# A decoder layer's retention: column-tiled products in one run per chunk, state in f16 halves, weight rows loaded a job ahead

## The chip, the cores and the metric

The kernel runs on one core of a Trainium2 chip, in one launch. The metric is the device time of an execution in microseconds, as a median over runs. The core has a matmul engine (TensorE; PE in the profile, with its weight loads as PEld) and three engines for elementwise work: VectorE (DVE), ScalarE (ACT) and GpSimd (POOL). SyncE (SP) issues nearly all DMAs, in order. Each engine takes its instructions in the order in which the program holds them and waits on semaphores for the others.

## The reference, cut to what matters

One decoder layer over x of 4 sequences of 1024 tokens, 512 wide: causal attention with head gates, then retention over a context, then a feed-forward with faked 8-bit quantisation; each is added to its input and normalised. The change concerns the second part.

```python
def _L0_xattn_ref(query, key, value, W_Q, W_K, W_V, g_w, g_b, out_w, out_b):
    q = jnp.einsum('bld,hde->bhle', query, W_Q)
    k = jnp.einsum('bld,hde->bhle', key, W_K)
    v = jnp.einsum('bld,hde->bhle', value, W_V)
    q = _xpos(q, downscale=False)
    k = _xpos(k, downscale=True)
    sim = jnp.einsum('bhnd,bhsd->bhns', q, k) * _decay_mask(L, H)[None]
    ret = jnp.einsum('bhns,bhsd->bhnd', sim, v)
    mu = ret.mean(axis=-1, keepdims=True)
    var = ret.var(axis=-1, keepdims=True)
    ret = (ret - mu) / jnp.sqrt(var + GN_EPS)
    ret = ret.transpose(0, 2, 1, 3).reshape(B, L, D)
    gate = jax.nn.silu(query @ g_w.T + g_b)
    return ret * gate @ out_w.T + out_b

x = _layernorm(x + _L0_attn_ref(x, ...))
x = _layernorm(x + _L0_xattn_ref(x, ctx, ctx, ...))
x = _layernorm(x + _L0_ffn_ref(x, ...))
```

`_decay_mask` is gamma to the power n - s on and below the diagonal, with one gamma for each of 16 heads of 32 columns.

## The kernel before

It has three parts, one after the other on the same core. The **attention** (`main`, `coarse`, `proj` and others) takes batch by batch, four groups of four heads each. The **retention** takes the 4096 tokens in 16 units of 256 tokens, each of two chunks of 128. The **feed-forward** first multiplies by the gate and up weights, then by the down weights; those weights are quantised during the retention.

Precision comes from pairs: a value is split into a high and a low f16 half, and a product is three f16 matmuls (`mm3g`, lines 196 to 198: high by high, high by low, low by high). Some products take f32 operands instead.

*A retention chunk* (`core`, line 999). For each of four groups `o` of four heads: four f16 score products `pst` (L1018), k and q stacked as three parts of 32 rows; a causal mask on DVE, which writes `sm` in f32 (L1020); and, one group later, `intra`: one f32 product of the carried state with `qtf`, the f32 copy of the transposed q (L1008), and four column-tiled f32 products, one for each head, `vv` against `sm` (L1012). Column-tiled means that each writes 32 of the 128 output partitions (`tile_position`). All of a chunk goes to one PSUM bank, `po`, which ACT copies to `rf` (L1040). The new state is `pkv` = k by v (L1029), plus the old state on DVE (L1034), times the decays on POOL (L1035).

*The tail of a chunk*: `tail_a` transposes `rf`, forms the norm over each head (with a power on POOL, L1059) and multiplies by the gate; `tail_b` multiplies by the output weights, adds the residual row `r` (loaded at L1047 into one of `NRB` = 4 buffers), normalises and stores (L1086).

*The projections of the next unit* (`stage1`: `kv`, then `qg`): k and v from the context, rotation tables on DVE and POOL, transposes to `kt` and `qt`. `q_trans` copies its PSUM tile to `qtf` on ACT (L335), then to the f16 high half (L336), and DVE forms the low half (L337). `k_stack` and `q_stack` write the halves to DRAM (`khl_d`, `qhl_d`, L263) and read them back stacked, in three loads each (`sk`, L266).

*Weight jobs* (`wjobs`, line 1088): 38 jobs that quantise the feed-forward weights. Each loads its row block into `fw`, one buffer (L1093, L1105), takes the maximum on DVE (L1095, L1111), quantises on ACT (L1126), casts, transposes on PE, copies and stores.

The order of the work is made by `gmerge`: each stream of work yields an estimated cost after each piece, divided by the stream's weight (`W_CORE`, `W_S1`, `W_F`, `W_TA`...), and the stream that is least far along emits its next piece. A scheduler in the build then settles the order on each engine. Tiles with the same tag share buffers; a new tile waits until the old one in its buffer has been read. `together` adds a dependence, so that a group of column-tiled matmuls isn't started before its last input is there; the attention already uses it.

Of the kernel before, what the change touches and what calls it, by code (L numbers as in the profile page):

```python
# [18 lines left out]
P = 128  # L19
# [11 lines left out]
XS = 1024.0  # L31
MS = 256.0
KEEP = 5
NHS = 6
# [23 lines left out]
WB = 16e3  # L58
TW = 0.307
QW = 15125.0  # L60
# [9 lines left out]
ATLP = 0  # L70
NRB = 4
X_S = 215.2
# [3 lines left out]
WBY = 250  # L76
X_P = 151.7
D_NM = 163.1
W_PR = 20760.0
W_G = 8800.0  # L80
W_X = 10160.0
W_S = 10250.0
W_BE = 11480.0
W_F = 2293.0
W_S1 = 33600.0
W_CORE = 5199.0
W_TA = 1605.0
D_TA = 504.8
# [49 lines left out]
def decoder_kernel(ctx: ExitStack, tc: tile.TileContext, a, c, out):  # L138
# [102 lines left out]
    ktab = []  # L241
    qtab = xp.tile([P, NT, 2, HD // 2], F32, name="qtab")
    etab = xp.tile([P, H], F32, name="etab")
    cmask = xp.tile([P, P], F32, name="cmask")
    FULL = [P, H, HD // 2, 2]
# [62 lines left out]
    def q_tiles(u, tiles):  # L308
        s = un[u]
        s.update(tiles)  # L310
        s["qtf"] = xp.tile([P, KC, UT], F32, tag="suf", name="qtf", bufs=2)
        s["sg"] = {}
# [9 lines left out]
    def q_proj(u, t, ps, **mm):  # L322
        s = un[u]
        p = ps.tile([P, 512], F32, name="pq", **mm)
        yield from mm3g(p, [lambda k, i_=i_: s["xs"][t][:, i_, k, :] for i_ in range(2)], [lambda k, w_=w_: w_[:, k, :] for w_ in bw[2]], KC, 213)
        cs = [qtab[:, tt(u, t), i, None, :].unsqueeze(3).to_broadcast(FULL) for i in range(2)]
# [22 lines left out]
    with ExitStack() as es:  # L349
# [64 lines left out]
        nc.vector.tensor_scalar_mul(ident_m, ident, -1.0 / MS)  # L414
        bsel = cp.tile([3, 3, P], F32, name="bsel")
        tiny = cp.tile([P, 1], F32, name="tiny")
# [59 lines left out]
        def gates(bs):  # L476
            n = len(bs)
            hid = wk_.tile([P, 8, 4], F32, tag="g_hid", name="g_hid", bufs=1)[:, :, 0:n]
            xw = wk_.tile([P, KC, 32], F32, tag="g_xw", name="g_xw", bufs=1)
            nc.gpsimd.memset(xw, 0.0)  # L480
# [340 lines left out]
        def weights_b():  # L821
# [17 lines left out]

            for t, nm in ((qtab, "qtab"), (etab, "etab"), (cmask, "cmask")):  # L840
                nc.sync.dma_start(out=t, in_=c[nm])
# [110 lines left out]
    with ExitStack() as es:  # L952
# [46 lines left out]
        def core(u, t):  # L999
            s = un[u]  # L1000
            kk, vv, qtf, ksk, qsk = (s[k] for k in ("kk", "vv", "qtf", "ksk", "qsk"))
            first, last = tt(u, t) == 0, tt(u, t) == NT - 1
            state = carry.get("state")
            po = ps.tile([P, KC, P], F32, tag="po", name="po", bufs=1)

            def intra(o, sm):
                if not first:
                    nc.tensor.matmul(po[:, o, :], lhsT=state[:, o, :], rhs=qtf[:, o, tk(t)], start=True, stop=False)  # L1008
                with tc.high_priority():
                  for h in range(4):  # L1010
                    r = slice(32 * h, 32 * h + 32)
                    nc.tensor.matmul(po[r, o, :], lhsT=vv[:, t, o * P + 32 * h:o * P + 32 * h + 32], rhs=sm[:, h, :], start=first, stop=True, tile_position=(0, 32 * h))  # L1012

            prev = None
            for o in range(KC):
                pst = ps.tile([P, 4, P], F32, tag="st", name="pst", bufs=2)
                for h in range(4):
                    nc.tensor.matmul(pst[:, h, :], lhsT=ksk[:, h, o, tk(t)], rhs=qsk[:, h, o, tk(t)], start=True, stop=True)  # L1018
                sm = wk_.tile([P, 4, P], F32, tag="sm", name="sm", bufs=NSM)
                nc.vector.tensor_tensor(out=sm, in0=pst, in1=cmask[:, None, :].to_broadcast([P, 4, P]), op=ALU.mult)  # L1020
                yield 213
                if prev is not None:
                    intra(*prev)
                    yield 480
                prev = (o, sm)
            if not last:
# [6 lines left out]
                else:  # L1033
                    nc.vector.tensor_tensor(out=ns, in0=pk, in1=state, op=ALU.add)  # L1034
                    nc.gpsimd.tensor_tensor(out=ns, in0=ns, in1=maskg, op=ALU.mult)  # L1035
                carry["state"] = ns
                yield 853
            intra(*prev)
            rf = s["rf", t] = wk_.tile([P, KC, P], F32, tag="rf", name="rf", bufs=2)
# [27 lines left out]
        def tail_b(u, t):  # L1067
# [18 lines left out]
            nc.sync.dma_start(out=x2_d[ti * P:(ti + 1) * P, :], in_=r)  # L1086

        def wjobs():
# [9 lines left out]
            for o in range(KC):  # L1098
                w3 = wk_.tile([P, 3], F32, tag="wm3", name="wm3")
                wm = wk_.tile([P, 1], F32, tag="wm", name="wm")  # L1100

                def load(o, j):
                    n = min(512, I - 512 * j)
                    w = wk_.tile([P, D], F32, tag="fw", name="fw", bufs=1)
                    nc.sync.dma_start(out=w[:, :n], in_=a["w_down"][o * P:(o + 1) * P, 512 * j:512 * j + n])  # L1105
                    return w, n

                def bound(o=o, w3=w3, wm=wm):
                    for j in range(3):
                        w, n = load(o, j)  # L1110
                        nc.vector.tensor_reduce(out=w3[:, j:j + 1], in_=w[:, :n], axis=AX.X, op=ALU.max, apply_absolute_value=True)  # L1111
                    nc.vector.tensor_reduce(out=wm, in_=w3, axis=AX.X, op=ALU.max)
                yield bound
                for j in range(3):
                    def job(o=o, j=j, wm=wm):
                        w, n = load(o, j)
                        wfinish(w, wm, 2 * NI + o, n, lambda pt_sb: nc.sync.dma_start(out=wT_d["w_down"][:, 4 * j:4 * j + n // P, o * P:(o + 1) * P], in_=pt_sb[:, :n // P, :]))
# [234 lines left out]
def _constants():  # L1352
# [25 lines left out]
    c["ktab"] = ktab.reshape(NT, P, 2, D // 2).transpose(1, 0, 2, 3).astype(f)  # L1378
    c["etab"] = (EPS * gam[None, :] ** (-2.0 * p[:, None])).astype(f)
    mg = np.zeros((P, KC, P), f)  # L1380
# [48 lines left out]
```

## Time and profile before

| | us |
|---|---|
| runs of the kernel | 1962.6, 1973.27, 1976.05 |
| median | 1973.27 |
| the profiled execution | 1978.85 |
| its span, first to last instruction | 1977.1 |
| mean granted TensorE clock | 0.979 |

The profile is of one execution. Line numbers (L1012) are those of the kernel before; `out<-in` names tiles; "x8" counts records that follow each other. An f32 matmul of 128 columns leaves two records, an f32 transpose one. Records of matmuls overlap, since matmuls are pipelined: the cost of one is read from its start to the start of the next. Busy time of 40 slices of the span, in tenths, shows the three parts:

```profile
PE   7689899999999999998889999999999999799996
DVE  4567766677766777678886777787777767798888
ACT  5655555555555555555553323333223322454375
POOL 1075566756667656766553455445554545200066
```

The retention is the stretch from the 22nd digit to the 34th, where ACT is least busy.

### The profile page before, as it was taken

The page shows a single profiled execution, that of the slowest core. Times are in us where ns is not written, and L with a number is a line of the kernel's source. Part 1 is how long each engine was busy: PE and PEld are TensorE (multiplying, and loading weights), DVE is VectorE, ACT ScalarE, POOL GpSimd, SP SyncE. Part 2 cuts the span into 40 slices and gives each one's busy share as a digit, 9 for nine tenths or more (in the row PEclk, how much of TensorE's full clock was granted, in tenths as well). Part 3 has the DMA queues.
Part 4 walks back from the last instruction along what each step waited for, and adds up shares of the span by engine and source line. Part 5 has one row for each costly group of instructions (what it writes and reads, how often), then busy time and mean ns, then how long its engine had stood idle before and what let it go on. Part 6 is the DMA issues. An engine that isn't in the chain of part 4 may idle for free. (4 is left out here: it accounts for less than half of the span.)

```text
span 1977.1 us, 34827 instructions
## 1 busy us (share of the span) xinstructions
PE 1832.6 (93%) x13456; PEld 968.2 (49%) x13456; DVE 1455.4 (74%) x2455; ACT 918.2 (46%) x1496; POOL 1015.4 (51%) x962
## 2 busy tenths in 40 slices
PE   7689899999999999998889999999999999799996
PEld 4444445444445444554434555555555555344432
DVE  4567766677766777678886777787777767798888
ACT  5655555555555555555553323333223322454375
POOL 1075566756667656766553455445554545200066
PEclk9899999999999999999999999999999999899999
DMA  9612222212123112223137454454545444561076
GB/s 272 192 45 67 82 73 68 84 60 81 54 68 97 62 55 65 73 81 129 44 95 223 136 149 139 147 158 134 153 143 150 120 120 144 176 231 34 0 240 229
DMA packets 149720, 231.00 MB, mean 117 GB/s; under 512 B 34479, under 2 KB 58674, under 8 KB 148914
## 3 DMA queue, kind: packets, MB, share of 16 engines
q1 hardware_dynamic: 148978, 227.72, 38.0%
q8 instruction: 106, 1.74, 0.4%
q10 hardware_dynamic: 576, 1.05, 0.1%
q14 instruction: 60, 0.49, 0.1%
HBM read 156.89 MB, written 71.70 MB: 116 GB/s over the span
## 5 line engine op out<-in xcount | busy, mean ns | idle before, releaser
L693 POOL TENSOR_TENSOR acc<-acc,pt 128x384 f32<-128x384 f32 (+3 forms) x436 | 441.0, 1042 | 244.5 <-ACT pt L707 146.2
L637 DVE TENSOR_REDUCE m<-pco 128x2 f32<-128x1024 f32 (+3 forms) x384 | 356.9, 950 | 128.5 <-PE pco L636 71.3
L707 ACT ACTIVATE pt<-pst 128x1024 f32<-128x1024 f32 (+3 forms) x320 | 240.6, 766 | 179.5 <-PE pst L706 102.4
L633 PE MATMUL pco<-kst,qst 96*128 96x512 f16 (+3 forms) x768 | 186.0, 332 | 28.6 <-DMA qst<-qhl_d 15.7
L703 PE MATMUL pst<-qst,kst 97*128 97x512 f16 (+3 forms) x768 | 187.6, 331 | 9.1 <-DVE m L637 4.9
L1324 POOL TENSOR_TENSOR r<-r,xt 128x512 f32<-128x512 f32 x28 | 38.4, 1383 | 196.2 <-DVE r L1321 186.6
L688 PE MATMUL av<-pt,v 128*32 128x512 f32 (+3 forms) x1280 | 131.0, 482 | 8.7 <-ACT pt L707 7.9
L633 PEld LDWEIGHTS <-qst 96*128 96x128 f16 x768 | 63.7, 99 | 120.2 <-issue 83.7
L1059 POOL TENSOR_TENSOR rs<-var,neghalf 128x16 f32<-128x16 f32 x32 | 93.6, 2925 | 46.9 <-DVE var L1057 26.4
L703 PEld LDWEIGHTS <-kst 97*128 97x128 f16 x768 | 59.4, 98 | 104.0 <-issue 83.2
L1253 PEld LDWEIGHTS <-slab_c 128*128 128x128 bf16 x704 | 68.3, 98 | 78.4 <-issue 1.4
L196 PE MATMUL pqk<-xh,slab_a 128*128 128x512 f16 x256 | 97.1, 384 | 8.7 <-ACT xh L399 5.9
L693 DVE TENSOR_TENSOR acc<-acc,pt 128x512 f32<-128x512 f32 (+3 forms) x102 | 96.5, 963 | 8.7 <-POOL acc L693 4.7
L197 PE MATMUL pqk<-xl,slab_a 128*128 128x512 f16 x256 | 98.0, 383 | 0.0
L198 PE MATMUL pqk<-xh,slab_a 128*128 128x512 f16 x256 | 97.8, 382 | 0.0
L196 PE MATMUL pkv<-slab_b,ch 128*128 128x512 f16 x256 | 97.0, 379 | 0.4 <-DVE dn L732 0.4
L197 PE MATMUL pkv<-slab_b,ch 128*128 128x512 f16 x256 | 97.0, 379 | 0.0
L198 PE MATMUL pkv<-slab_b,cl 128*128 128x512 f16 x256 | 97.0, 379 | 0.0
L1256 ACT ACTIVATE sl<-pw_gate,sgx 128x512 f32<-128x512 f32 x88 | 60.1, 684 | 76.3 <-PE pw_gate L1253 74.7
L196 PE MATMUL pv<-slab_a,xh 128*128 128x128 f16 x512 | 92.0, 221 | 3.4 <-ACT slab_a L170 2.4
L197 PE MATMUL pv<-slab_a,xh 128*128 128x128 f16 x512 | 92.0, 221 | 1.2 <-DVE slab_a L171 1.2
L1020 DVE TENSOR_TENSOR sm<-pst,cmask 128x512 f32<-128x512 f32 x128 | 85.3, 679 | 10.5 <-PE pst L1018 9.2
(299 smaller groups left out, 4595.7 us busy)
## 6 DMA issues: line engine op xcount, KB each, us to landing
xt<-x_d SPq DMA_DIRECT2D x63, 256.0 KB, 3.1
xf<-in_xT_dram SPq DMA_DIRECT2D x48, 256.0 KB, 2.8
kst<-khl_d SPq DMA_DIRECT2D x48, 256.0 KB, 4.0
qst<-qhl_d SPq DMA_DIRECT2D x96, 128.0 KB, 3.8
sk<-qhl_d SPq DMA_DIRECT2D x48, 256.0 KB, 3.8
sk<-khl_d SPq DMA_DIRECT2D x48, 256.0 KB, 4.0
khl_d<-khl SPq DMA_DIRECT2D x16, 512.0 KB, 2.8
xr<-in_x_dram SPq DMA_DIRECT2D x32, 256.0 KB, 2.7
```

The costliest lines, as they stand in the source:

```text
L196: nc.tensor.matmul(ps, lhsT=lh(k), rhs=rh(k), start=k == 0, stop=False)
L197: nc.tensor.matmul(ps, lhsT=lh(k), rhs=rl(k), start=False, stop=False)
L198: nc.tensor.matmul(ps, lhsT=ll(k), rhs=rh(k), start=False, stop=k == n - 1)
L633: nc.tensor.matmul(p[:, j, :n], lhsT=qst[0:96, half, h + j, i * P:(i + 1) * P], rhs=ks[0:96, h + j, 512 * part:512 * part + n], start=True ...
L637: nc.vector.tensor_reduce(out=m[:, h:h + 2, i, 1 - half + part], in_=p[:, :, :n], axis=AX.X, op=ALU.max)
L688: together(nc.tensor.matmul(av[32 * h:32 * h + 32, lo:], lhsT=v[:, kt, 32 * h:32 * h + 32], rhs=pt[:, h, lo:], start=kt == 0, stop=kt == n ...
L693: last["acc"] = eng.tensor_tensor(out=acc[:, h:h + hb, lo:], in0=acc[:, h:h + hb, lo:], in1=pt[:, h:h + hb, lo:], op=ALU.add)
L703: nc.tensor.matmul(p[:, j, lo:], lhsT=ks[:, h + j, kt * P:(kt + 1) * P], rhs=qst[:, g, h + j, lo:], start=True, stop=kt < 4 * g)
L707: last[kt] = nc.scalar.activation(pt[:, h:h + 2, lo:], p[:, :, lo:], AF.Exp)
L1020: nc.vector.tensor_tensor(out=sm, in0=pst, in1=cmask[:, None, :].to_broadcast([P, 4, P]), op=ALU.mult)
L1059: nc.gpsimd.tensor_tensor(out=rs, in0=var, in1=neghalf, op=ALU.pow)
L1253: nc.tensor.matmul(p, lhsT=wT[nm][:, k, i * P:(i + 1) * P], rhs=xqT[g][:, k, :], start=k == 0, stop=k == KC - 1)
```

## The change

Its core:

```diff
+VS = 16.0
-TW = 0.307
+TW = 0.2345
-NRB = 4
+NRB = 3
-X_P = 151.7
-D_NM = 163.1
+X_P = 219.7
+D_NM = 211.1
-W_X = 10160.0
+W_X = 15000.0
-W_F = 2293.0
-W_S1 = 33600.0
-W_CORE = 5199.0
-W_TA = 1605.0
+W_F = 1773.0
+W_S1 = 22680.0
+W_CORE = 12560.0
+W_TA = 3398.0
...
-        cl = xp.tile([P, KC, UT], F16, tag="qk32", name="cl", bufs=2)
+        cl = xp.tile([P, KC, UT], F16, tag="qk32", name="cl")
...
-        nc.scalar.activation(un[u]["vv"][:, t, :], p, AF.Copy, scale=1.0 / XS)
+        nc.scalar.activation(un[u]["vv"][:, t, :], p, AF.Copy, scale=VS / XS)
...
-        nc.scalar.copy(s["qtf"][:, :, tk(t)], pt)
         nc.scalar.copy(qh, pt)
...
-                f = xp.tile([P, 512], F32, tag="qk32", name="qk32", bufs=2)
+                f = wk_.tile([P, 512], F32, tag="xr", name="qk32", bufs=2) if b == 0 and ot < 3 else xp.tile([P, 512], F32, tag="qk32", name="qk32")
...
-            def intra(o, sm):
-                if not first:
-                    nc.tensor.matmul(po[:, o, :], lhsT=state[:, o, :], rhs=qtf[:, o, tk(t)], start=True, stop=False)
-                with tc.high_priority():
-                  for h in range(4):
-                    r = slice(32 * h, 32 * h + 32)
-                    nc.tensor.matmul(po[r, o, :], lhsT=vv[:, t, o * P + 32 * h:o * P + 32 * h + 32], rhs=sm[:, h, :], start=first, stop=True, tile_position=(0, 32 * h))
-            prev = None
+            sms = []
             for o in range(KC):
                 pst = ps.tile([P, 4, P], F32, tag="st", name="pst", bufs=2)
                 for h in range(4):
                     nc.tensor.matmul(pst[:, h, :], lhsT=ksk[:, h, o, tk(t)], rhs=qsk[:, h, o, tk(t)], start=True, stop=True)
-                sm = wk_.tile([P, 4, P], F32, tag="sm", name="sm", bufs=NSM)
-                nc.vector.tensor_tensor(out=sm, in0=pst, in1=cmask[:, None, :].to_broadcast([P, 4, P]), op=ALU.mult)
+                if o == 0:
+                    sm2 = xp.tile([P, 2, 4, P], F32, tag="suf", name="sm2", bufs=2)
+                sm = sm2[:, o] if o < 2 else wk_.tile([P, 4, P], F32, tag="sm", name="sm", bufs=NSM)
+                masked = nc.vector.tensor_tensor(out=sm, in0=pst, in1=tab["mask"][:, None, :].to_broadcast([P, 4, P]), op=ALU.mult)
+                sms.append(sm)
                 yield 213
-                if prev is not None:
-                    intra(*prev)
-                    yield 480
-                prev = (o, sm)
+            if not first:
+                for o in range(KC):
+                    for i, (x_, y_) in enumerate(((0, 0), (0, 1), (1, 0))):
+                        nc.tensor.matmul(po[:, o, :], lhsT=state[1][:, x_, o, :], rhs=qt[:, y_, o, tk(t)], start=o == 0 and i == 0, stop=False)
+                yield 640
+            with tc.high_priority():
+                for o in range(KC):
+                    for h in range(4):
+                        r = slice(32 * h, 32 * h + 32)
+                        together(nc.tensor.matmul(po[r, o, :], lhsT=vv[:, t, o * P + 32 * h:o * P + 32 * h + 32], rhs=sms[o][:, h, :], start=first, stop=first or o == KC - 1, tile_position=(0, 32 * h)), masked)
...
+                nh = wk_.tile([P, 2, KC, P], F16, tag="state16", name="state16")
+                nc.scalar.copy(nh[:, 0], ns)
+                nc.gpsimd.tensor_tensor(out=nh[:, 1], in0=ns, in1=nh[:, 0], op=ALU.subtract)
+                carry["state"] = ns, nh
...
+        def fetch():
+            src = next(loads, None)
+            if src:
+                w = wk_.tile([P, D], F32, tag="fw", name="fw", bufs=2)
+                nc.sync.dma_start(out=w[:, :src[1]], in_=src[0])
+                loaded.append((w, src[1]))
+        def take():
+            if not loaded:
+                fetch()
+            w = loaded.pop(0)
+            fetch()
+            return w
...
-                        w = wk_.tile([P, D], F32, tag="fw", name="fw", bufs=1)
-                        nc.sync.dma_start(out=w, in_=a[nm][i * P:(i + 1) * P, :])
+                        w, _ = take()
```

In words: `qtf` and its copy go; the state is kept in f32 for the recurrence and also as two f16 halves, and its product with q becomes three f16 products that add into the same bank; the sixteen column-tiled products of a chunk come last, in one run, tied to the last mask. `vv` is scaled by 16, and the constant table of the norm's epsilon by its square. Weight rows get two buffers, and a job's load is issued a job ahead; `loads` lists the blocks in the order in which the jobs take them. The space comes from tables that take over buffers of the attention's gates (`bsel`, `g_xw`), from `NRB`, and from `qk32`, which keeps one of two buffers; the masked scores of the first two groups go where `qtf` was (`suf`). `W_S` changes too, but no stream uses it.

More of the change, by code (lines that the diff above doesn't have):

```diff
@@ L76 @@
 WBY = 250
-X_P = 151.7
-D_NM = 163.1
+X_P = 219.7
+D_NM = 211.1
 W_PR = 20760.0
 W_G = 8800.0
-W_X = 10160.0
-W_S = 10250.0
+W_X = 15000.0
+W_S = 10990.0
 W_BE = 11480.0
-W_F = 2293.0
-W_S1 = 33600.0
-W_CORE = 5199.0
-W_TA = 1605.0
+W_F = 1773.0
+W_S1 = 22680.0
+W_CORE = 12560.0
+W_TA = 3398.0
 D_TA = 504.8
@@ L241, in decoder_kernel @@
     ktab = []
-    qtab = xp.tile([P, NT, 2, HD // 2], F32, name="qtab")
+    tab = {}
     etab = xp.tile([P, H], F32, name="etab")
-    cmask = xp.tile([P, P], F32, name="cmask")
     FULL = [P, H, HD // 2, 2]
@@ L310, in q_tiles @@
         s.update(tiles)
-        s["qtf"] = xp.tile([P, KC, UT], F32, tag="suf", name="qtf", bufs=2)
         s["sg"] = {}
@@ L325, in q_proj @@
         yield from mm3g(p, [lambda k, i_=i_: s["xs"][t][:, i_, k, :] for i_ in range(2)], [lambda k, w_=w_: w_[:, k, :] for w_ in bw[2]], KC, 213)
-        cs = [qtab[:, tt(u, t), i, None, :].unsqueeze(3).to_broadcast(FULL) for i in range(2)]
+        cs = [tab["q"][:, tt(u, t), i, None, :].unsqueeze(3).to_broadcast(FULL) for i in range(2)]
         xpos(p, cs[0], cs[1], s["qq"][t])
@@ L414, in decoder_kernel @@
         nc.vector.tensor_scalar_mul(ident_m, ident, -1.0 / MS)
-        bsel = cp.tile([3, 3, P], F32, name="bsel")
+        bsel = xp.tile([3, 3, P], F32, tag="bsel", name="bsel")
         tiny = cp.tile([P, 1], F32, name="tiny")
@@ L478, in gates @@
             hid = wk_.tile([P, 8, 4], F32, tag="g_hid", name="g_hid", bufs=1)[:, :, 0:n]
-            xw = wk_.tile([P, KC, 32], F32, tag="g_xw", name="g_xw", bufs=1)
+            xw = xp.tile([P, KC, 32], F32, tag="g_xw", name="g_xw")
             nc.gpsimd.memset(xw, 0.0)
@@ L838, in table @@
                 ktab.append(t)
-            for t, nm in ((qtab, "qtab"), (etab, "etab"), (cmask, "cmask")):
+            tab["q"] = xp.tile([P, NT, 2, HD // 2], F32, tag="bsel", name="qtab")
+            tab["mask"] = xp.tile([P, P], F32, tag="g_xw", name="cmask")
+            for t, nm in ((tab["q"], "qtab"), (etab, "etab"), (tab["mask"], "cmask")):
                 nc.sync.dma_start(out=t, in_=c[nm])
@@ L1000, in core @@
             s = un[u]
-            kk, vv, qtf, ksk, qsk = (s[k] for k in ("kk", "vv", "qtf", "ksk", "qsk"))
+            kk, vv, qt, ksk, qsk = (s[k] for k in ("kk", "vv", "qt", "ksk", "qsk"))
             first, last = tt(u, t) == 0, tt(u, t) == NT - 1
@@ L1033, in core @@
                 else:
-                    nc.vector.tensor_tensor(out=ns, in0=pk, in1=state, op=ALU.add)
+                    nc.vector.tensor_tensor(out=ns, in0=pk, in1=state[0], op=ALU.add)
                     nc.gpsimd.tensor_tensor(out=ns, in0=ns, in1=maskg, op=ALU.mult)
-                carry["state"] = ns
+                nh = wk_.tile([P, 2, KC, P], F16, tag="state16", name="state16")
+                nc.scalar.copy(nh[:, 0], ns)
+                nc.gpsimd.tensor_tensor(out=nh[:, 1], in0=ns, in1=nh[:, 0], op=ALU.subtract)
+                carry["state"] = ns, nh
                 yield 853
-            intra(*prev)
             rf = s["rf", t] = wk_.tile([P, KC, P], F32, tag="rf", name="rf", bufs=2)
@@ L1086, in tail_b, with wloads @@
             nc.sync.dma_start(out=x2_d[ti * P:(ti + 1) * P, :], in_=r)
+        def wloads():
+            for nm in ("w_gate", "w_up"):
+                for i in range(NI):
+                    yield a[nm][i * P:(i + 1) * P, :], D
+            for o in range(KC):
+                for _ in range(2):
+                    for j in range(3):
+                        n = min(512, I - 512 * j)
+                        yield a["w_down"][o * P:(o + 1) * P, 512 * j:512 * j + n], n
+        loads, loaded = wloads(), []
+        def fetch():
[10 more added lines that the diff above has]
+            return w
         def wjobs():
@@ L1100, in wjobs, with bound @@
                 wm = wk_.tile([P, 1], F32, tag="wm", name="wm")
[L1102 to L1108, printed above, removed]
+                def bound(w3=w3, wm=wm):
                     for j in range(3):
-                        w, n = load(o, j)
+                        w, n = take()
                         nc.vector.tensor_reduce(out=w3[:, j:j + 1], in_=w[:, :n], axis=AX.X, op=ALU.max, apply_absolute_value=True)
@@ L1115, in job @@
                     def job(o=o, j=j, wm=wm):
-                        w, n = load(o, j)
+                        w, n = take()
                         wfinish(w, wm, 2 * NI + o, n, lambda pt_sb: nc.sync.dma_start(out=wT_d["w_down"][:, 4 * j:4 * j + n // P, o * P:(o + 1) * P], in_=pt_sb[:, :n // P, :]))
@@ L1378, in _constants @@
     c["ktab"] = ktab.reshape(NT, P, 2, D // 2).transpose(1, 0, 2, 3).astype(f)
-    c["etab"] = (EPS * gam[None, :] ** (-2.0 * p[:, None])).astype(f)
+    c["etab"] = (EPS * VS * VS * gam[None, :] ** (-2.0 * p[:, None])).astype(f)
     mg = np.zeros((P, KC, P), f)
```

## The prediction

> **What bounds the kernel now.** I read the totals first, then the three stretches of the span that the two stage borders cut out (1062.6 us: first score product `pst` of the retention; 1703.5 us: the matmul `pmax` that opens the feed-forward), then the waits of TensorE in the middle stretch, then its instructions in order of time.
>
> ```profile
> PE 1832.6 (93%) x13456; PEld 968.2 (49%) x13456; DVE 1455.4 (74%) x2455; ACT 918.2 (46%) x1496; POOL 1015.4 (51%) x962
> ```
> ```profile
> 0.00:1062.60 1062.60, 975.47 (x7749) 497.85 (x7750) 747.52 (x1126) 580.49 (x985) 630.38 (x636) 0.98 0.31 91
> 1062.60:1703.50 640.90, 613.25 (x4513) 358.07 (x4512) 472.79 (x901) 190.10 (x322) 319.92 (x267) 0.98 0.48 142
> 1703.50:1977.10 273.60, 243.90 (x1196) 112.27 (x1195) 235.10 (x428) 147.60 (x189) 65.09 (x59) 0.96 0.47 158
> ```
> Columns: length, busy us of PE, weight loads, DVE, ACT, POOL, then granted clock, DMA share, GB/s. The retention (second row) is where nearly all of the change lies: PE is busy 96% of it, DVE 74%, POOL 50%, ACT 30%. So a PE slot saved there shortens the span, and work moved to ACT or POOL has room. What PE waits for there:
>
> ```profile
> PE po L1012 <- DVE sm L1020: 5.8, 6, 2.2
> PE pst L1018 <- DMA sk<-qhl_d: 4.4, 4, 1.9
> PE pout L196 <- ACT zh L170: 4.1, 6, 1.2
> ```
> Total us, times, longest. These are small; the stage is a queue of matmuls. The slots, from three places of the timeline (start, length, group):
>
> ```profile
> 1213.89 0.39 PE L1008 MATMUL po<-qtf,state 128*128 128x128 f32 x2
> 1214.21 0.43 PE L1012 MATMUL po<-sm,vv 128*32 128x128 f32 x8
> 1214.57 0.49 PE L1008 MATMUL po<-qtf,state 128*128 128x128 f32 x2
> ```
> ```profile
> 1230.61 1.04 PE L318 MATMUL ptx<-ident,x 128*128 128x128 f32 x8
> 1231.58 0.65 PE L1012 MATMUL po<-sm,vv 128*32 128x128 f32 x16
> 1232.16 0.39 PE L196 MATMUL pout<-wo,zh 128*128 128x512 f16 x1
> ```
> ```profile
> 1440.87 0.38 PE L1008 MATMUL po<-qtf,state 128*128 128x128 f32 x2
> 1441.09 0.38 PE L196 MATMUL pkv<-slab_b,ch 128*128 128x512 f16 x1
> 1452.82 0.61 PE L1018 MATMUL pst<-sk 96*128 96x128 f16 x8
> 1453.26 0.38 PE L196 MATMUL pgt<-wg,xs 128*128 128x512 f16 x1
> ```
> Lengths overlap, so I use start to start. One f32 state product (two records) takes 1441.09-1440.87 = 0.22 us. Eight f16 products of 128 columns, each with its own weight load, take 0.44: 0.055 each. A column-tiled group of four heads (8 records) starts at 1214.21, though the state product before it ends its slot at 1213.89+0.22 = 1214.11, and lets the next start at 1214.57: 0.45 in all (two decimals; over all 116 such groups the median is 0.451). Two groups in one run (16 records): 0.67 from the end of the transposes (1230.61 plus eight of 0.11) to 1232.16. So a further group in a run costs 0.22, and entering and leaving the tiled mode 0.23.
>
> **The change part by part.**
>
> Column-tiled runs. Before: 116 single groups and 6 doubles, 116x0.451 + 6x0.668 = 56.3 us. In the changed program's instruction order all 32 chunks have their 16 tiled matmuls next to each other: 32x(0.23+4x0.2185) = 35.4. Saved: **-20.9**, all of it PE slots.
>
> State products. Before 112 f32 at 0.22: 25.0 us. After 336 f16 (high by high, high by low, low by high) at 0.055 to 0.057 (the 128x128 f16 products `pv` of the attention average 0.057 with a load each): 19.0. **-6.0**. Bound above: if no load overlapped, the 0.098 us of the load record each, 32.9, +8; I take the f16 rows, the same shape beside the same work.
>
> The Trainium skill ("TensorE: Matmul & The Clock Gate", section Back-to-back issue gap) speaks against this part: it gives about 81 ns for a sustained load-and-matmul pair of 128 columns. By it the estimate for the states would be 336x0.081 = 27.2, a loss of 2 instead of a gain of 6; the slot of 55 ns on the `pst` row above decides.
>
> Masks. A run now waits for the mask of the last of its four score tiles (`together`), and everything behind it in PE's order waits too. In the new order 3.5 to 6.0 us of other matmuls stand between that score product and the run in 30 chunks (before, per group, 0.7 to 21.8); the last two chunks have 0.9 and 0.2. The trace puts the mask's end 1.65 us (median) after its product, 4.2 at nine in ten. So of the 5.8 us waited now I let 2 go: **-2** (bounds -5 to +8, a quarter us per chunk).
>
> Recurrence. Product `pkv`, DVE add, POOL mask, and now an ACT copy to f16 and a POOL subtract (28 of each: about 0.59 and 1.27 us, by rows of those engines at 128x512). Before, state is ready 3.0 us after `pkv`; now about 5.0. PE has 5.6 to 18 us of other matmuls before the first state product of the next chunk, so the new wait is covered: **+0.5**. If one 2.9-us `rs` power (L1059) stands before the subtract on POOL, 7.9 against those distances leaves ten chunks short, +10; nothing below zero, since nothing waited here. What is queued behind a late state product is all of PE. ACT loses the 32 `qtf` copies (0.58 each) and gains 28: free.
>
> Hand-over of q. Before a unit's first score product, `qt` goes to DRAM and back in three loads `sk`:
>
> ```profile
> 1339.73 0.37 SPq L263 DMA_DIRECT2D qhl_d<-qt  x1
> 1344.62 0.52 SPq L1096 DMA_DIRECT2D w_up_d<-fs  x1
> 1345.23 1.54 SPq L266 DMA_DIRECT2D sk<-qhl_d  x3
> ```
> From the last q transposition to the last landing it takes 10.5 us (unit 11: 1499.2 to 1509.7), 11.6 (unit 2), 12.9 (unit 5), 14.6 (unit 15); the lines show why: the store was issued at 1339.73 and takes 2.8, but SP's queue held the loads until 1345.23 behind a weight store. Other units had their product after 10.4 to 11, so 11.3 is typical. The dropped `qtf` copy stood first on ACT: 10.7 from now on. The redrawn weights let the projections (W_S1 33600 to 22680) come later beside the core (W_CORE 5199 to 12560): the matmuls that cover the hand-over shrink from 9.8-12.0 us to 8.1, 8.5, 10.7, 11.1, 11.3, 10.6, 10.0, 9.7, 10.9, 11.2, 11.3, 10.4, 10.9, 11.2, 9.4 in units 1 to 15. What is short of 10.7 adds up to 8.2, less 4.4 waited now: **+4** (bounds -4.4, and +34 at 12.9 less 0.6 rounded up).
>
> Weight rows ahead. DVE waited 34.9 us for `fw` (25.2 before L1095, 9.7 before L1111). DVE is no bound; the PE waits that come after its weight work are 2.2 us. I take **-1** (0 to -10). Loads on SP keep their number; with two buffers each waits for a quantisation a job back.
>
> Tail. The last chunk's masks end, then 1.1 us of tiled matmuls instead of 0.45 go before the copy that starts the last norm: **+0.7**.
>
> Attention. Its stream weights (W_X, X_P, D_NM) shift single instructions by up to 3 us of PE work, the gates by 15 earlier; totals stay. `qk32` loses a buffer: a write would wait for the subtract before it. In the trace 6 of the projections after the first three heads start 0.3 to 0.7 us before that subtract ends, 2.6 us together, on ACT. **0** (bounds -4 and +4). The tables' new tags belong to tiles that the gates use last, at 206 us; the tables are loaded near 1000. `NRB` 3: in both instruction orders a residual row's load stands 1 to 6 places behind the store that frees its buffer on SP, so no new kind of wait comes; the load is one chunk later, and POOL, which already waits 84.5 us for these rows (L1048), may hold the state's steps behind it: inside the +10 of the recurrence.
>
> Sum: -20.9-6.0-2+0.5+4-1+0.7 = -24.7. The profiled execution took 1978.85 us (span 1977.1 and 1.75 around it): 1954.1. The median of the runs is 5.6 lower, so I forecast **1948 us**.
>
> **The rivals.** (1) *Much of it goes into the hand-over*: at 11.5 us the covers above fall 17.2 short, +13 instead of +4, and with the recurrence at half its bound (+5): 1948+9+4.5 = 1962. For: SP blocks, and DVE serves the low half late. Against: 11.3 is today's typical value with `qtf` in it. (2) *Slower: the hand-over becomes the clock of each unit.* If SP's order, one queue for weight rows ahead, residual rows and `sk`, brings every unit to what unit 15 shows, 13.9 without `qtf`, the shortfall is 53.2, +48.8: 1948-4+48.8 = 1993. From 12.4 on (shortfall 31) it eats the whole gain. Against: another transfer stands between the store and the `sk` loads in 6 of 15 units in both orders, and in the trace it made such units late by 0 to 4.5 us. (3) *The redraw costs the attention time*, ACT held by `qk32` and so the exponentials: 0.4 us (the mean of those six) in each of the 52 later writes with PE behind it, +21: 1969. (4) *The runs aren't one in the silicon's sense*, the drain being paid per PSUM column block: -20.9 falls to 0, 1969. Against: the 16-record line above.
>
> **How the numbers follow.** Forecast 0.60, rival 1 0.16, rival 2 0.09, rival 3 and rival 4 together 0.15. About 1% (20 us) is what a measurement of this kernel can tell from no change: runs of before lie 13 us apart. The forecast's own spread (about 10 each way by its bounds) puts a fifth of it inside 1%; rivals 1, 3 and 4 lie mostly inside. Faster 0.58, same 0.31, slower 0.11. Range: low, with -4.4 at the hand-over and -4 in the attention, 1936; high, to the inner rivals, 1973.
>
> **What would show it.** Right: the retention stretch lasts about 616 us instead of 641, PE starts 32 records of the tiled product in 1.1 us per chunk, state products start 55 ns apart, the stretch before 1062 stays within 4. Wrong: waits of `pst` for `sk` over 15 us; state products waiting for POOL; mean start-to-start of the state products above 80 ns; a longer attention with ACT waiting for POOL at the `qk32` writes.

## The result and the profile after

| | before | changed |
|---|---|---|
| median of 20 runs, us | 1971.56 (1962.6 to 1977.58) | 1977.13 (1971.51 to 1981.72) |
| ratio, 95% interval | 1 | 1.003 (1.0019 to 1.004) |
| profiled execution: span, us | 1977.1 | 1975.3 |
| attention / retention / feed-forward, us | 1062.8 / 640.4 / 273.9 | 1072.6 / 628.0 / 274.7 |
| mean granted clock | 0.979 | 0.972 |

The forecast was 1948 in 1936 to 1973, so the time lies 29 us above it and 4 above the range. The profiled execution took 1977.1 us (span and 1.75), its median, where that of before lay 7 above its own; against the prediction's sum for a profiled execution, 1954.1, it is 23 us late. The other 6 of the 29 are the 5.6 us that the forecast took off for a profile above its median: the changed kernel's isn't. The three stages of the changed kernel, with the columns of the prediction's table (length; busy us of PE, weight loads, DVE, ACT, POOL; clock, DMA share, GB/s):

```profile
0.00:1072.57 1072.57, 979.12 (x7750) 500.92 (x7751) 752.52 (x1125) 575.59 (x982) 628.76 (x636) 0.98 0.29 89
1072.57:1700.59 628.02, 590.08 (x4623) 354.96 (x4621) 472.19 (x902) 193.98 (x321) 354.35 (x295) 0.97 0.50 147
1700.59:1975.30 274.71, 243.47 (x1172) 112.72 (x1196) 237.61 (x428) 147.62 (x189) 65.08 (x59) 0.95 0.46 158
```

PE's busy time in the retention falls by 23 us (613.25 to 590.08), but the stretch only by 12; and the attention, which was to stay, is 10 longer. First the slots, from the changed kernel's timeline of PE (start, length, group):

```profile
1302.22 0.38 PE L197 MATMUL pout<-wo,zh 128*128 128x512 f16 x1
1302.53 1.08 PE L1026 MATMUL po<-sm,vv 128*32 128x128 f32 x32
1303.54 0.66 PE L332 MATMUL ptq<-ident,qq 128*128 128x128 f32 x4
```
```profile
1411.20 0.83 PE L1020 MATMUL po<-qt,state 128*128 128x128 f16 x12
1411.87 0.38 PE L197 MATMUL pq<-slab_b,xs 128*128 128x512 f16 x1
```

From the end of the slot before (1302.22 and 0.22) to 1303.54 a run of 32 takes 1.10 us; the median of all 32 runs is 1.105 (1.106 was foreseen). Twelve f16 state products take 1411.87-1411.20 = 0.67, or 0.056 each. So all 27 us of slots are gone, as the sum had it. What PE waits for in the retention now (total us, times, longest):

```profile
PE pst L1010 <- DMA sk<-qhl_d: 7.1, 4, 3.1
PE pmax L1219 <- DVE gx_m L1217: 4.2, 1, 4.2
PE pst L1010 <- issue: 4.1, 3, 2.6
PE bt L1055 <- DVE z L1064: 3.6, 2, 2.5
PE pst L1010 <- DVE sm L1014: 3.0, 6, 0.8
...
PE pst L1010 <- DMA fw<-in_w_gate_dram: 1.4, 1, 1.4
...
PE pst L1010 <- DMA w_gate_d<-fs: 1.3, 1, 1.3
```

The rows of `pst` behind `sk`, "issue", `fw` and `w_gate_d` are one thing, the pause before a unit's first score product, put down to whichever semaphore came last. To see it whole I took, for every record of PE, its start less the start of the record before and that record's slot (128 columns f16 0.056, 512 columns 0.216, f32 twice that, a tiled record 0.0273 and 0.2325 for a run), and summed the excess by the product that starts late. The last row is the time in which the granted clock was 0.5, halved: the most that the slower clock can have cost.

```
excess in the retention, us        before   changed
score products pst                    8.6      22.5
pout (behind zh)                      9.0       5.8
state products                        6.5       1.0
transposes bt (behind rf, z)          0.9       4.4
pkv (projections of k and v)          0.2       3.6
all others                           14.9      17.9
sum                                  40.1      55.2
clock: throttled time / 2, at most    9.5      17.6
```

27.2 us of slots saved less 15.1 of excess returned is 12.1, all but 0.3 of what the retention gained (640.4 to 628.0). 13.9 of the 15.1 stand at the score products. That share is rough: half of each 0.2325 is booked at a run's entry and half at its exit, and booked at one end alone `pst` before would be 5.2 or 11.9; the sums stay.

### The profile page after: what moved, and what is told of

Read it like the earlier page. It is cut to its first block, busy times and chain, and to the rows that moved or that the text cites. A ratio compares the mean times of both kernels' runs of the same rounds, so it can differ in the third digit from the quotient of the medians.

```text
span 1975.3 us, 34972 instructions
## 1 busy us (share of the span) xinstructions
PE 1812.7 (92%) x13544; PEld 968.6 (49%) x13568; DVE 1462.3 (74%) x2455; ACT 917.2 (46%) x1492; POOL 1048.2 (53%) x990
## 3 DMA queue, kind: packets, MB, share of 16 engines
q8 instruction: 107, 1.75, 0.4%
## 5 line engine op out<-in xcount | busy, mean ns | idle before, releaser
L701 PE MATMUL pst<-qst,kst 97*128 97x512 f16 (+3 forms) x768 | 186.9, 332 | 12.1 <-DVE m L635 8.1
L755 POOL TENSOR_TENSOR xr<-xr,bo 128x512 f32<-128x512 f32 x32 | 42.0, 1312 | 126.5 <-DMA xr<-in_x_dram 120.6
L197 PE MATMUL pv<-slab_a,xh 128*128 128x128 f16 x512 | 91.6, 222 | 5.1 <-ACT slab_a L171 2.7
L1051 POOL TENSOR_TENSOR r<-r,obias 128x512 f32<-128x512 f32 x32 | 40.9, 1280 | 99.8 <-DMA r<-x_d 59.9
```

The lines of the kernel that those rows point to most:

```text
L197: nc.tensor.matmul(ps, lhsT=lh(k), rhs=rh(k), start=k == 0, stop=False)
L701: nc.tensor.matmul(p[:, j, lo:], lhsT=ks[:, h + j, kt * P:(kt + 1) * P], rhs=qst[:, g, h + j, lo:], start=True, stop=kt < 4 * g)
```

## The experiments

Four kernels split the change into its attention and its retention side. All times are medians; ratios are to the kernel before on the same chip, with 95% intervals. In the four rounds of runs the kernel before itself had medians of 1969.8 to 1973.9, so between rounds the ratios count for more than the medians. Stage lengths are of one profiled execution each.

**attn_as_before.** `qk32` gets two buffers again, one for each half of a sequence's tokens, and four weights of the attention their old values:

```diff
-TW = 0.2345
+TW = 0.307
-X_P = 219.7
-D_NM = 211.1
+X_P = 151.7
+D_NM = 163.1
-W_X = 15000.0
+W_X = 10160.0
...
+                f = (xp if t else wk_).tile([P, 512], F32, tag="qk32" if t else "qk32b", name="qk32", bufs=1)
```

> The changed kernel with the attention's part of the change undone: qk32 has two buffers again and TW, X_P, D_NM and W_X their old values; the retention is as changed. In the changed kernel the stretch up to the first score product of the retention lasts 1072.6 us instead of 1062.8, and the retention 628 instead of 640. Theory: these are two separate effects, so the attention falls back to 1063 (within 3), the retention stays at 628 (within 4), and the time is about 1967, a ratio to before near 0.998. Rival: the attention's loss comes from elsewhere (tables and gate tiles in other buffers, or only chance in the order); then it stays at 1068 or more and the time at 1974 to 1978.

1965.3 us, 0.9961 (0.9944 to 0.9978): 0.4% faster than before, and 12 us below the changed kernel. Attention 1056.6, retention 628.9, in an execution that was the fastest of ten (1958.8). The attention's part of the loss is real.

**qk32_two**: the buffers alone, with the new weights.

> The changed kernel with two buffers for qk32 in the attention, all emission weights as redrawn. Theory (one buffer makes ACT wait for POOL's subtract, and the exponentials behind it): the attention comes down by 6 to 10 us from 1072.6, the ACT waits for POOL at the qk32 writes go, time about 1969. Rival (the redrawn X_P, D_NM, W_X and TW cost it): the attention stays within 3 of 1072.6, time 1975 to 1978.

1985.6, 1.0071 (1.0047 to 1.0095). **attn_weights_old**: the four weights alone, with one buffer.

> The changed kernel with the old X_P, D_NM, W_X and TW, and one buffer for qk32. Theory of the single buffer: the attention stays within 3 of 1072.6 us, or gets longer, since the new weights were drawn for one buffer; time 1975 to 1980. Rival (the weights cost it): the attention comes down by 6 to 10, time about 1969.

1972.5, 0.9992 (0.9976 to 1.0007). So neither part works by itself: with two buffers the new weights cost 20 us (1985.6 against 1965.3), with one 5 (1977.1 against 1972.5); the second buffer gains 7 under the old weights and loses 8 under the new. From 1965.3 the changed kernel is reached by 7 for the buffer and 5 for the weights; by the profiles the weights lengthen the attention by 1 of these 5 (1071.4 to 1072.6). The buffer's part shows where rival 3 looked for it, in the waits of ACT in the changed kernel's attention, here with the waits of PE for ACT's `suf` and `qk`:

```profile
ACT qk L562 <- POOL khl L566: 15.4, 6, 3.5
PE psuf L609 <- ACT suf L614: 5.5, 1, 5.5
PE pqk L197 <- ACT qk L562: 3.4, 2, 3.1
```

The write of `qk32` waits for POOL's subtract that frees its only buffer. attn_weights_old has 12.8 us of such waits, the two kernels with two buffers none. How they reach TensorE isn't shown: ACT's exponentials stand behind these writes in its order, but PE's long waits for ACT (also in attn_weights_old, 6.9 and 4.2; in qk32_two 0.9 and 0.3) lie nearly all in the first 62 us, and the six waits of ACT in the changed kernel begin at 238.

**ret_weights_old**: the changed kernel with `W_F`, `W_S1`, `W_CORE` and `W_TA` of before.

```diff
-W_F = 1773.0
-W_S1 = 22680.0
-W_CORE = 12560.0
-W_TA = 3398.0
+W_F = 2293.0
+W_S1 = 33600.0
+W_CORE = 5199.0
+W_TA = 1605.0
```

> The changed kernel with the old W_F, W_S1, W_CORE and W_TA in the retention; the attention's instruction order is that of the changed kernel (1072.6 us). Theory: the redrawn weights put the next unit's projections later and shorten what covers the hand-over of q, so with the old ones the waits of the first score products for sk fall from about 15 us to about 6, and the retention goes from 628 to about 618 (time 1967). Rival: the redrawn weights are what the single run needs (masks ready, state ready); with the old ones the waits for masks and for the state grow by more than the hand-over gives, and the retention lasts 628 to 640 (time 1977 to 1988).

1994.2, 1.0109 (1.0085 to 1.0133), retention 648.7. My theory, that these weights cost time through the hand-over, fell: they are worth 17 us. With the old ones the new core has 27 us fewer slots than before and a retention 8 us *longer* than before's 640.4; the excess by the measure above is 75.6.

The next four took the retention apart, three of them on attn_as_before, to be free of the attention's loss.

**no_handover** and **before_no_handover**: only the first unit's query stack is read, so nothing waits for the later ones (and the output isn't the layer's); the transfers stay.

```diff
-        un[u]["qsk"] = stack(un[u]["qt"], hl_d["q", u % 2], (0, 1, 0), f"kst{(u + 1) % 2}", 1)
+        sk = stack(un[u]["qt"], hl_d["q", u % 2], (0, 1, 0), "kst0" if u else "kst1", 1); un[u]["qsk"] = un[0]["qsk"] if u else sk
```

> The version attn_as_before (1965.3 us), with every unit's score products reading the query stack of the first unit (its output is not the reference's: units 1 to 15 score the first unit's queries); the stack is still stored to DRAM and loaded again, but nothing waits for it. Theory A, what came back in the retention is the hand-over of q (pst waiting for sk, the weight loads queued ahead of it, and the throttled clock after those pauses): 1950 us or less, retention 629 down to 614 or less, other than slots 60 down to 45. Rival B, the waits for sk are only the 4 to 7 us that the waits show and the rest is spread over sm, z, fq: 1959 to 1963, retention 622 to 627.

> The kernel before with the same edit (units 1 to 15 score the first unit's queries). Theory A: the hand-over costs before only its 4.4 us of waits and little clock, so 1966 to 1969, retention 635 to 637. Rival B: the same gain as in the changed kernel, whatever that is.

1959.3 (0.9948, 0.9928 to 0.9968) and 1969.8 (0.9995, 0.998 to 1.0011): gains of some 3 us by the ratios and 6 by the medians, and of 0 to 1: nearer to B than to A. The scheduler puts the score products elsewhere when the wait is gone, so this is not the old order less a wait. In the profile the score products' excess falls from 23.6 to 9.9, but the sum only from 55.8 to 46.5. What stands there now (no_handover, waits of PE in the retention):

```profile
PE pst L1010 <- DVE sm L1014: 5.3, 6, 1.5
PE pmax L1219 <- DVE gx_m L1217: 4.2, 1, 4.2
PE ptz L1075 <- DVE z L1067: 3.6, 1, 3.6
PE pst L1010 <- DMA sk<-khl_d: 2.4, 1, 2.4
```

**runs_apart**: each run of 32 cut into four of 8, each behind its quarter's state products.

```diff
-            if not first:
-                for o in range(KC):
-                    for i, (x_, y_) in enumerate(((0, 0), (0, 1), (1, 0))):
-                        nc.tensor.matmul(po[:, o, :], lhsT=state[1][:, x_, o, :], rhs=qt[:, y_, o, tk(t)], start=o == 0 and i == 0, stop=False)
...
                 for o in range(KC):
+                    for i, (x_, y_) in enumerate(((0, 0), (0, 1), (1, 0))) if not first else (): together(nc.tensor.matmul(po[:, o, :], lhsT=state[1][:, x_, o, :], rhs=qt[:, y_, o, tk(t)], start=o == 0 and i == 0, stop=False), masked)
                     for h in range(4):
```

> attn_as_before with the 32 runs of 32 tiled matmuls cut into four of 8 each, the three f16 state products of a quarter ahead of each. Slots by the rows of before: 3 more entries and exits of 0.23 us in 32 chunks = +22. Theory C, the retention is a queue of slots and a slot saved is time saved: 1987 (+22). Rival D, a saved slot comes back as waits at the unit starts (only 12 of 27 us were gained), so slots put back are taken from those waits: 1972 to 1977 (+7 to +12).

1994.1, 1.0136 (1.0113 to 1.0159): 29 us slower than attn_as_before, 34 by the ratios. Theory C, and more than its slots: 28 chunks have a carried state and are cut, which makes 28x3x0.2325 = 19.5 of entries and exits. The timeline of that kernel shows what a chunk pays:

```profile
1228.74 0.34 PE L1024 MATMUL po<-qt,state 128*128 128x128 f16 x3
1229.02 0.43 PE L1027 MATMUL po<-sm,vv 128*32 128x128 f32 x8
1229.37 0.34 PE L1024 MATMUL po<-qt,state 128*128 128x128 f16 x3
1229.64 0.43 PE L1027 MATMUL po<-sm,vv 128*32 128x128 f32 x8
```

A quarter takes 1229.37-1228.74 = 0.63 us, of which 0.17 are the three state products and 0.46 the eight tiled records. What comes on top of the 19.5 isn't separated: with the cut the state products too wait for the chunk's last mask (`together`), which they don't in attn_as_before. The run is the part of the change that works, and its price in slots was right.

**s1_nudged**: `W_S1` 23000 for 22680, which changes which product stands at about a third of the places in PE's order in the retention.

> attn_as_before with one weight of the retention moved by 1.4% (W_S1 22680 to 23000), which leaves the instructions and reorders some of TensorE's queue in the retention. Theory E, the order decides little at this scale: within 3 us of 1965. Rival F, the weights are fitted to one order and any other costs: 1969 to 1978.

1965.6, 0.9975 (0.9961 to 0.9988): E. This reordering moved the time by less than a microsecond; one nudge doesn't speak for others.

**fw_one**: one buffer for the weight rows, each loaded in its own job.

```diff
-                w = wk_.tile([P, D], F32, tag="fw", name="fw", bufs=2)
+                w = wk_.tile([P, D], F32, tag="fw", name="fw", bufs=1)
...
             w = loaded.pop(0)
-            fetch()
```

> attn_as_before (1965.3 us) with one buffer for the weight rows and each loaded in its own job, as before. Theory: the look-ahead is worth nothing to TensorE (the prediction's -1, 0 to -10): 1964 to 1968, DVE waiting some 35 us for fw again, TensorE's waits behind fq within 3 us. Rival: the loads a job ahead sit in SP's queue before the query stack's loads and cost the hand-over, so taking them away gains: 1955 to 1961.

1968.3, 0.9976 (0.996 to 0.9992): 1.5 by the ratios, 3 by the medians, within both intervals. DVE waits 42.6 us for `fw` here and 26.9 in attn_as_before; PE hardly notices.

**states_f32**: fw_one with the f32 state products and `qtf` of before, and with six `sm` buffers in place of three and the two of `sm2`, which hold two groups each.

```diff
-                    for i, (x_, y_) in enumerate(((0, 0), (0, 1), (1, 0))):
-                        nc.tensor.matmul(po[:, o, :], lhsT=state[1][:, x_, o, :], rhs=qt[:, y_, o, tk(t)], start=o == 0 and i == 0, stop=False)
+                    for i in range(1):
+                        nc.tensor.matmul(po[:, o, :], lhsT=state[0][:, o, :], rhs=s["qtf"][:, o, tk(t)], start=o == 0 and i == 0, stop=False)
...
-                nh = wk_.tile([P, 2, KC, P], F16, tag="state16", name="state16")
-                nc.scalar.copy(nh[:, 0], ns)
-                nc.gpsimd.tensor_tensor(out=nh[:, 1], in0=ns, in1=nh[:, 0], op=ALU.subtract)
```

> fw_one with the f32 state products of before (112 of 0.22 us in place of 336 of 0.056), the qtf copies back and the state's ACT copy and POOL subtract gone; one run of 32 tiled matmuls as in the changed kernel. Theory by slots: +6 against fw_one. Rival, the shorter recurrence and POOL's free time give that back: -3 to +2 against fw_one.

1964.8, 0.9972 (0.9959 to 0.9985), against 1968.3 (0.9976) of fw_one: no slower. 6.3 us more of slots, 6.5 less excess (49.8 against 56.3), the retention 629.2 in both. The f16 halves brought nothing measurable.

**f32_ret_old**: states_f32 with the retention weights of before.

> states_f32 (1964.8 us: two qk32 buffers, attention weights of before, one buffer for weight rows, f32 states, one run per chunk) with the retention weights of before (W_F, W_S1, W_CORE, W_TA). With f16 states the old retention weights cost 17 us. Theory J, it is the longer way to the f16 state (ACT copy, POOL subtract) that the old order cannot take: 1963 to 1969. Rival K, it is the run, which waits for the mask of its last tile with all of a chunk's score products before it, whatever the state's format: 1977 to 1985.

1991.3, 1.0085 (1.0063 to 1.0106), retention 652.5: 22 (ratios) to 27 us (medians) above states_f32, beyond K's range, so the old order fails the one run whatever the state's format. The waits that appear (f32_ret_old, PE in the retention) are not mainly the run's own wait for its mask, which K supposed:

```profile
PE ptw L1152 <- DVE qt L335: 8.4, 5, 4.1
PE pout L197 <- ACT zh L171: 7.6, 8, 1.9
PE pst L1010 <- DMA sk<-qhl_d: 6.2, 3, 4.2
PE pst L1010 <- DVE sm L1014: 6.0, 7, 1.4
...
PE po L1026 <- DVE sm L1014: 2.1, 2, 1.9
```

Why the order of before lets these come late is open: no run separates moving the score products to the front from joining the tiled ones under the old weights.

**gates_last**: the next unit's two gate projections both behind its query stack.

```diff
             yield from q_trans(u, 0, ps, **tr)
-            if u < NU - 1:
-                yield from g_proj(u, 0)
             yield from q_trans(u, 1, ps, **tr)
             q_stack(u)
             if u < NU - 1:
+                yield from g_proj(u, 0)
                 yield from g_proj(u, 1)
```

> attn_as_before with both gate projections of the next unit emitted behind its query stack, so 2.6 us more of matmuls lie between the last query transposition and the first score product. Theory G, the hand-over's 15 us are distances too short by 0.5 to 3.3 us: 1955 to 1959, the pauses before the units' first score products down from 15 to under 5. Rival H, as with no_handover what is taken from that pause comes back as waits elsewhere (the transposition now waits for qq): 1962 to 1966.

1965.4, 0.9968 (0.9953 to 0.9982): nothing. The reason is not quite H's: the matmuls between the last query transposition and the first score product still add up to 8.4 to 10.4 us (8.1 to 11.3 in the changed kernel). The order that the build settles on did not lengthen that distance, the pauses still add up to 14.6 us, and so G was not tried by it.

**s1_27000**: `W_S1` between the two values.

> attn_as_before with W_S1 27000, between the 22680 of the changed kernel and the 33600 of before, so that the next unit's projections come earlier beside the core. Theory N, the distance that covers the hand-over of q grows again and its pauses (15 us in attn_as_before, 5.7 in before) shrink by half: 1956 to 1961. Rival O, the pauses go and others take their place, as with no_handover and gates_last: 1962 to 1970.

1961.3, 0.9927 (0.9906 to 0.9948): the fastest here that computes the layer. The pauses at the units' first score products add up to 6.8 us instead of 15.1; the retention is 623.5, the excess 50.4 against 55.8. Of 8.3 us taken from the pauses 5.4 stayed. So N holds in direction and place, O for a third of it. The waits of PE in its retention:

```profile
PE bt L1055 <- DVE z L1064: 7.7, 2, 6.1
PE pst L1010 <- DVE sm L1014: 7.6, 5, 2.6
PE pst L1010 <- DMA sk<-qhl_d: 3.5, 4, 1.7
```

Three runs looked for the one of the attention's weights that costs the time, all with two `qk32` buffers on attn_as_before: **attn_times_new** has `X_P` and `D_NM` of the changed kernel, **x_charge_new** `X_P` alone (the charge for a step that splits x), **norm_delay_new** `D_NM` alone.

> attn_as_before (two qk32 buffers) with X_P 219.7 and D_NM 211.1 of the changed kernel, W_X and TW of before. With all four new it was 1985.6, with none 1965.3. Theory: the two times inside the streams (the projection's step and the norm's delay) bring most of it, as they set when the exponentials and masks are emitted: 1978 to 1986. Rival: it is the stream weight W_X, which moves the other stream against the projections: 1964 to 1969 here.

> attn_as_before (1965.3 us) with X_P alone of the changed kernel: the charge for a step that splits x, 219.7 for 151.7. With D_NM new as well it was 1996. Theory L, this one does it, as it moves every later step of the projections' stream against the attention's: 1985 to 1996. Rival M, D_NM does it and this run stays at 1962 to 1969.

> attn_as_before (1965.3 us) with D_NM alone of the changed kernel: the distance charged between the reduction of the coarse maxima and the transposition that waits for it, 211.1 for 163.1. Theory L: 1962 to 1969. Rival M, the delay moves every pnm against the score products: 1985 to 1996.

1996.0 (1.0127, 1.0108 to 1.0147), 1975.9 (1.0006, 0.9991 to 1.0021) and 1995.1 (1.0097, 1.0076 to 1.0118). `D_NM` brings 27 (ratios) to 30 us (medians), as rival M had it; `X_P` alone brings 9 to 11, between L and M, and the two don't add up. `D_NM` is the charge between the reduction of the coarse maxima and the transposition `pnm`; raised by 48 it makes the attention stretch 1092.2 us long, with 23 us more excess than in attn_as_before at the coarse score products `pco` (64.1 against 41.2), of 36 in all; why a later `pnm` makes these late isn't shown. (attn_as_before's profile is a fast one: seven kernels with its order of PE in the attention have 1062.7 on average, and against that the attention is 30 longer, as by the medians.) How such a pause is paid shows at 650 us of norm_delay_new, first in PE's timeline, then in windows of 3.41 us (busy us of PE, weight loads, DVE, ACT, POOL; granted clock):

```profile
650.30 1.06 PE L686 MATMUL av<-acc,v 128*32 128x512 f32 x8
654.47 0.22 PE L631 MATMUL pco<-kst,qst 96*128 96x128 f16 x1 [3.10 <-DMA kst<-khl_d]
```
```profile
649.23:652.65 3.42, 2.13 (x19) 0.98 (x17) 0.62 (x2) 3.35 (x6) 1.61 (x3) 1.00 1.08 231
652.65:656.06 3.41, 1.08 (x12) 0.64 (x12) 0.42 (x1) 0.69 (x1) 2.69 (x3) 1.00 0.50 131
656.06:659.47 3.41, 3.41 (x21) 1.87 (x19) 1.74 (x3) 0.03 (x1) 0.93 (x2) 0.50 0.20 77
659.47:662.88 3.41, 3.41 (x36) 2.32 (x34) 3.04 (x5) 2.40 (x6) 1.05 (x2) 1.00 0.00 0
```

PE stands still for 3.1 us behind a load of `kst`; the window that follows is granted half the clock, though PE is busy all through it, and costs up to 1.7 us more. Half of the throttled time adds up in the attention to 39.3 us in norm_delay_new and to 17.1 to 25.6, on average 21.5, in those seven kernels: at most 18 of the 30 us.

## Why the forecast failed

By the profiled executions 23 us of the forecast are missing: 10 in the attention, 12 in the retention, under 1 in the feed-forward. Three steps failed: the attention was put at nothing and cost 10 to 12 us; the state products were to save 6 us of time and saved slots alone; and the hand-over of q was put at +4 and measures +9.7. The last two make 11.7 of the retention's 12, but they were measured separately and need not add. Of the prediction's own signs, the run's 1.1 us and the state products' slot came as for right; the longer attention with ACT waiting at `qk32`, and the pauses of `pst` behind `sk` (15.4 us, the sign being 15), came as for wrong.

*Column-tiled runs, -20.9*: right in slots (32 of 1.105 us), and in the new order these slots are time (cutting the runs puts back 19.5 us of slots and costs 29).

*State products, -6.0*: the slots were right (0.056 each, not 0.081), the time was not. states_f32 gives the same time without them. The step that failed is taking every saved PE slot as time: it held for the run, but these 6 us came back as excess. Whether the longer recurrence or POOL's busier queue takes them isn't separated; state products themselves wait only 0.4 us for POOL, so *recurrence, +0.5* was right as a direct wait.

*Masks, -2*: about right by the direct waits. `po` waits 1.2 us instead of 5.8; score products now wait 3.0 for `sm` buffers and score tiles.

*Hand-over of q, +4*: the mechanism was right, the size was not. The pauses add up to 15.4 us against 5.7 before, +9.7 (the 4.4 of the prediction was only the part put down to `sk`). The mean way from the last query transposition to the last landing is 10.9 us, near the 10.7 foreseen, but by luck: before it was 10.9 too, not 11.3, so the 0.6 of the dropped copy doesn't show. The covering matmuls came out as listed. But the way varies from 7.5 to 13.3 us from unit to unit, and I subtracted one typical value from each cover. A unit that is early earns nothing; one that is late pays. With the ways of before (8.6 to 14.9), each less the 0.6 of `qtf`, averaged over the same covers, the shortfall is 12.0 rather than 8.2; with each unit's own new way and cover it is about 16. (Two bounds of this working were off too: +34 belongs to 12.9 us, not to that less 0.6, which gives 29.2-4.4 = +25; and a shortfall of 31, less the 4.4, doesn't yet eat a gain of 28.7.) Unit 1 shows what a late one looks like in the changed kernel, on DVE, on SP and on PE:

```profile
1105.12 0.68 DVE L335 TENSOR_TENSOR qt<-ptq,qt 128x512 f16<-128x512 f32 x1
```
```profile
1105.83 0.38 SPq L263 DMA_DIRECT2D qhl_d<-qt  x1
1106.30 0.43 SPq L1107 DMA_DIRECT2D fw<-in_w_gate_dram  x1
1108.95 1.28 SPq L266 DMA_DIRECT2D sk<-qhl_d  x3
```
```profile
1110.84 0.40 PE L1152 MATMUL ptw<-ident_b,fq 128*128 128x128 bf16 x4 [0.52 <-DVE wsc L1143]
1114.38 1.01 PE L1010 MATMUL pst<-sk 96*128 96x128 f16 x8 [3.14 <-DMA sk<-qhl_d]
```

The last transposition ended at 1100.1, but the low half of q is only done at 1105.8, 5.7 us later; in the 15 units this first part takes 1.5 to 5.7 us, and much of the spread lies there, in ACT's and DVE's queues. The three loads go out at 1108.95 as soon as the store has landed, and PE has nothing else for 3.14 us. A second part of the term was missing altogether: at such pauses the clock halves. Stretches at half clock stand at the three longest (units 1, 9 and 15, at 1112, 1437 and 1669 us). Throttled time over 2 went from 9.5 to 17.6 us in the retention and from 20.5 to 25.6 in the attention; over the whole span from 42.4 to 56.0, 13.6 at most. The attention's part of that says little, as kernels with one order there have 17.1 to 25.6.

*Weight rows ahead, -1, and tail, +0.7*: right, as far as the runs can tell (fw_one).

*Attention, 0 (-4 to +4)*: wrong. It cost 12 us by the medians: 7 for the buffer and 5 for the weights on the way from attn_as_before. Counting how far each instruction moves, and finding that the totals stay, said nothing about which products would be late. The price in rival 3 (ACT held at 52 writes, +21) was too high (six writes wait, 15.4 us) and its place right for ACT's wait. One pair of profiles would not have shown this: seven kernels with one and the same order of PE in the attention have attentions of 1056.6 to 1068.4 us, mean 1062.7. The changed kernel and ret_weights_old, which share theirs, have 1072.6 and 1070.7, and the medians of the four kernels above agree.

*The redrawn retention weights* were treated as a cost alone (shorter covers). They are worth 17 to 27 us to the one run, and without them the change would have been slower, 1994. The slots were free to be saved only in an order drawn for them; that whole condition was missing from the sum. Rivals 1 and 3 were written as alternatives to each other; parts of both came together.

## What to carry to other kernels

Price a wait that recurs by its spread, not by its typical length: the shortfall of each occurrence counts, and the early ones give nothing back. Take an edit of buffers or stream weights in a stage that "only shifts" as unknown, with a bound of its own, and split a change by stage before judging it: here the retention gained 12 us by the profiles (attn_as_before is 7 faster than before by the medians), the attention lost 12, and the retention's part alone, with `W_S1` at 27000, is 0.7% faster than before (0.9927, 0.9906 to 0.9948). In these runs a slot taken from a full engine was time only as long as the order left that engine something else to do at each wait.

## What the hardware did that was not expected

The granted clock falls to 0.5 in whole windows of 3.41 us, on a grid that each execution places differently. I laid that grid over eight of the profiles and summed, for each window that began at full clock, how long PE had no slot running in the window before. After more than 2.0 us of standing still 130 of 152 windows ran at half the clock, after less 11 of 4227. The stillness need not be one pause: ahead of 898.4 us in norm_delay_new 2.06 us were enough, of which the longest pause was 1.6. The Trainium skill ("TensorE: Matmul & The Clock Gate", Part 1: The HAM clock gate) gives a free-running window of 3413 ns, which these records agree with; its advice of no gaps above about 3 us, in the same page's section Why this matters for your kernels, is too generous here. A pause of 2 to 3 us, of the sort that a hand-over through DRAM leaves, can so cost up to 1.7 us on top, or nothing, by where it falls on the grid; that would make some of the spread between executions of one kernel, which no run here tests.

Entering and leaving the column-tiled mode cost 0.23 us whatever the length of the run: 8 records 0.451, 16 records 0.67, 32 records 1.105.
